# A four-layer Perceiver kernel: ones rows through GpSimd's queue, key tiles cleared three blocks ahead, value copies on ScalarE, queries in four groups

## The chip, the cores and the metric

The kernel runs on one core of a Trainium2 chip. The metric is the device time of one execution in microseconds (us). TensorE is called PE here, VectorE DVE, ScalarE ACT and GpSimd POOL, as in the profile; SyncE (SP) only issues DMA transfers. PEld is TensorE's weight load.

## The reference

A state `x` of 128 rows by 256 passes four layers; each has a cross-attention to 12544 context rows, a self-attention variant and a feed-forward part, and each part's result is added to `x`:

```python
x = x + _L0_xattn_ref(_layernorm(x, axis=-1), ctx_1024, mask_BxS2_ik0, ...)
...
x = x + _L1_xattn_ref(ctx_1024, ctx_1024, _layernorm(x, axis=-1), fside_SxS2_0, fside_BxS2_0, ...)
...
x = x + _L2_xattn_ref(_layernorm(x, axis=-1), ctx_1024, ctx_1024, ...)
...
x = x + _L3_xattn_ref(_layernorm(x, axis=-1), ctx_1024, ctx_1024, mask_Bx1x1xS2_fk0, ...)
```

The four cross-attentions have the same core, with 16 heads of 16 numbers; as layer 0 has it:

```python
q = _split_heads(hidden_states @ q_w.T + q_b)
k = _split_heads(context @ k_w.T + k_b)
v = _split_heads(context @ v_w.T + v_b)
scores = jnp.einsum('bhqd,bhkd->bhqk', q, k) / jnp.sqrt(jnp.float32(HD))
mask = (attention_mask > 0)[:, None, None, :]
scores = jnp.where(mask, -jnp.inf, scores)
probs = jax.nn.softmax(scores, axis=-1)
ctx = jnp.einsum('bhqk,bhkd->bhqd', probs, v)
```

Layer 0 masks keys, layer 1 adds a full 128 x 12544 table and a row to the scores, layer 2 has no mask, layer 3 adds a row. The keys and values of all layers depend on the context alone, not on `x`. Layer 1's self-attention is a delta rule with convolutions, layer 2's a masked attention, and layer 2's feed-forward part is in fixed point with a GELU made of straight pieces.

## The kernel before, in words

The parts are named l0x, l0a, l0f, l1x, ... l3f (x cross-attention, a self-attention, f feed-forward) and run in this order. Everything is float32.

**Projection jobs.** The context's keys and values are projected in small jobs, 50 for keys and 49 for values for each of the four cross-attentions, in one list (`projections`, L155). A context block is 1024 rows (13 blocks, the last of 256); it is loaded by SyncE's queue, 1 MB, into one of two buffers (`load`, L184). A key job makes 128 x 512 keys on PE, ACT moves them from PSUM to SBUF (L209), and after a half block POOL's queue stores them to HBM (L212). A value job makes the values of 256 rows with eight matmuls (L226, run by `mm`, L315). They are copied from PSUM into a staging tile by ACT if `self.side` is set (L232), else by DVE (L234). Two jobs share a staging tile, whose ones columns POOL writes first (L223), and POOL's queue stores it (L237); there are two staging tiles. So a job's parts use PE, ACT or DVE, POOL and two DMA queues.

**Who runs the jobs.** In a cross-attention, as many jobs as the next steps need are run at once, and more by `rate` (0.9 a step in the first pass of l2x and l3x). Outside, `one` (L127) runs `self.share` jobs each time it hands out a PSUM bank; l1_attn, l2_attn and l2_ffn run jobs of later layers so. PSUM's eight banks are handed out in turn (L135).

**A cross-attention** (`cross`, L355). The norm of `x` is transposed, and the queries of all 16 heads are made in one bank, then scaled into four tiles `qb` (L381 to L392), one for each unit of four heads. A unit makes two passes over the keys, 25 steps of 512 keys each: the first takes the maxima of the scores (`score_s`: matmuls L483, DVE maxima L496, or L491 where layer 1 adds its table), the second makes the scores again, transposed, with the maximum taken off (`score_t`: L533), their exponentials on ACT (L546), and products with the values (L588). The second pass trails the first by 27 steps (`lead`), so that during the first 27 steps of a cross-attention there are only score steps and projection jobs (called the first pass below), and later both passes of neighbouring units side by side.

**Key tiles.** A score matmul multiplies 32 rows for a head: a row of ones, a row of the mask, 16 of keys, and zeros. The 17 tiles of 1024 keys by 128 rows (four heads) are made ready by `clear(n)` (L406): POOL zeroes a tile (L409), and SyncE's queue writes the four ones rows (L410, 16 KB). `fetch_k` (L420) is called two steps ahead; for each new block b it runs the jobs up to that block, calls `clear` so that tiles up to b + 2 exist, and issues on SyncE's queue the mask rows (L432) and four loads of keys (L437), and for layer 1 the side table (L442). Each tile is cleared once a cross-attention; later blocks reuse the tiles.

**Order.** The main loop of `cross` runs under a manual schedule: every engine and queue gets its instructions in the order in which the program writes them, and each of them works through its own in that order. Elsewhere the framework orders the instructions.

Of the kernel before, what the change touches and what calls it, by code (L numbers as in the profile page):

```python
# [10 lines left out]
F32 = mybir.dt.float32  # L11
# [7 lines left out]
P = 128  # L19
# [3 lines left out]
SB = 1024  # L23
ST = 512
NSB = -(-S2 // SB)
NST = -(-S2 // ST)
# [51 lines left out]
class Net:  # L78
# [276 lines left out]
    def cross(self, name, side=False, project=True, rate=()):  # L355
# [4 lines left out]
        nc, tc = self.nc, self.tc  # L360
        self.share, self.side = 0.0, side
        width = WIDTH[name]
        units = 16 // width
        lead = NST + 2
        batch = 4 // width
        behind = batch if width == 4 else batch + 1
        with ExitStack() as es:
            pool = es.enter_context(tc.tile_pool(name=f"{name}_p", bufs=1))
# [7 lines left out]
            def rows(u):  # L376

                at = 32 * (width * u % 4)
                return slice(at, at + 32 * width)

            ps = self.bank(f"{name}_q")  # L381
            for g in range(4):
                self.mm(ps[:, g * P : (g + 1) * P], [wq[:, c, g * P : (g + 1) * P] for c in range(2)],
                        [xnT[:, c, :] for c in range(2)])
            qb = []
            for u in range(units):
                g, r = width * u // 4, rows(u)
                q = pool.tile([P, P], F32, name=f"{name}_qb{u}", tag=f"qb{u}")
                nc.vector.tensor_scalar(out=q[r, :], in0=ps[r, g * P : (g + 1) * P],
                                        scalar1=self.col(f"{name}_qb")[r, g : g + 1],  # L390
                                        scalar2=0.25, op0=ALU.add, op1=ALU.mult)
                qb.append(q)  # L392
            lows = []
            for i in range(2):
                low = pool.tile([P, P], F32, name=f"{name}_low{i}", tag=f"low{i}")
# [10 lines left out]
            def clear(n):  # L406
                while len(kts) < min(held, n + 1):
                    t = kp.tile([P, SB], F32, name=f"{name}_kt{len(kts)}", tag=f"kt{len(kts)}")
                    nc.gpsimd.memset(t, 0.0)  # L409
                    nc.sync.dma_start(out=t[0::32, :],  # L410
                                      in_=self.io["ones"][:, :SB].to_broadcast([4, SB]))
                    kts.append(t)
                while len(vts) < nv:
                    n = SB // P * 17 * width
                    t = kp.tile([P, n + 15], F32, name=f"{name}_vt{len(vts)}",
                                tag=f"vt{len(vts)}")
                    nc.gpsimd.memset(t[:, n:], 0.0)
                    vts.append(t)

            def fetch_k(k):  # L420

                u, i = divmod(k, NST)
                if u >= units:
                    return
                s, m = i * ST, min(ST, S2 - i * ST)
                if s % SB == 0:
                    b = s // SB
                    self.until(name, b, "k")
                    n = min(SB, S2 - b * SB)
                    clear(NSB * u + b + 2)  # L430
                    t = kts[(NSB * u + b) % held]
                    nc.sync.dma_start(  # L432
                        out=t[1::32, :n],
                        in_=self.mask_rows[name][:, s : s + n].to_broadcast([4, n]))
                    for j in range(width):
                        at, h = 32 * j + 2, width * u + j
                        nc.sync.dma_start(out=t[at : at + 16, :n],  # L437
                                          in_=self.kx[name, b][16 * h : 16 * h + 16, :])
                    kt[u, b] = t
                if side:  # L440
                    f = ep.tile([P, ST], F32, name=f"{name}_f{k}", tag="f", bufs=3)
                    nc.sync.dma_start(out=f[:, :m], in_=self.io["fside"][:, s : s + m])  # L442
                    ft[k] = f
# [171 lines left out]
            with tc.manual_schedule():  # L615
                for k in (0, 1):
                    fetch_k(k)
                for at in range(total + lead + 3):
                    fetch_k(at + 2)
                    fetch_v(at + 2 - lead)  # L620
                    ke = at - lead if 0 <= at - lead < total else None
                    km = at if at < total else None
                    scores(ke, km)
                    if 0 < at <= total and at % NST == 0:
                        lower(at // NST - 1)


                    left = sum(1 for (n, _, _), _ in self.jobs if n == name)
                    goal = min(n_k, 2 * (at + 6))
                    if at >= lead - 6:  # L630
                        goal = min(n_own, n_k + 2 * (at - lead + 7))
                    self.pump(min(left, max(0, goal - (n_own - left))))
                    phase = max(0, at - 2) // NST
                    due += rate[phase] if phase < len(rate) else 0.0
                    while due >= 1.0:
                        self.pump(1)
                        due -= 1.0


                    while waiting:  # L640
                        u, i = divmod(waiting[0], NST)
                        n = NST - i if NST - i < 2 * batch else batch
                        last = waiting[0] + n - 1
                        if ke is not None and ke - last < behind - batch + 1:
                            break
                        if last > waiting[-1]:
                            break
                        values(waiting[:n])
                        waiting = waiting[n:]
                    if ke is not None:  # L650
                        waiting.append(ke)
                    u, i = divmod(at - lead - 2 - NST, NST)
                    if i == 0 and 0 <= u < units:
                        finish(u)
# [119 lines left out]
    def l1_attn(self):  # L774

        nc = self.nc
        H, HD = 4, 64
        with self.tc.tile_pool(name="l1a", bufs=1) as pool, \
                self.tc.tile_pool(name="l1a_r", bufs=2) as rp:
# [146 lines left out]
            for h, parts in enumerate((((0, 0), (1, 1)), ((1, 2), (2, 3)),  # L926
                                       ((3, 0), (4, 1)), ((4, 2), (5, 3)))):
                q = (h % 2) * HD
# [62 lines left out]
    def l1_ffn(self):  # L991

        nc = self.nc
        E = 8
        with self.tc.tile_pool(name="l1f", bufs=1) as pool, \
                self.tc.tile_pool(name="l1f_h", bufs=2) as hp:
# [67 lines left out]
    def l2_attn(self):  # L1064

        nc = self.nc
        with self.tc.tile_pool(name="l2a", bufs=1) as pool:
            w = self.weight(("w_l2a", None)).rearrange("p (c f) -> p c f", c=2, f=1024)
            xn, xnT = self.normed(pool, "l2a")
            xs = [xnT[:, c, :] for c in range(2)]  # L1070
            qk = []
            for i, nm in enumerate("qk"):
                ps = self.one(f"l2a_{nm}")
                for f in range(2):
                    at = i * D + f * P
                    self.mm(ps[:, f * P : (f + 1) * P], [w[:, c, at : at + P] for c in range(2)],
                            xs)
                t = pool.tile([P, 2, P], F32, name=f"l2a_{nm}T", tag=f"{nm}T")
                nc.vector.tensor_copy(t.rearrange("p c t -> p (c t)"), ps[:, :D])
                qk.append(t)  # L1080
            ps = self.one("l2a_v")
            self.mm(ps[:, :D], xs, [w[:, c, 512:768] for c in range(2)])
            v = pool.tile([P, D], F32, name="l2a_vs", tag="v")
            nc.scalar.copy(v, ps[:, :D])
            ps = self.one("l2a_s")
            self.mm(ps[:, :P], [qk[0][:, c, :] for c in range(2)],
                    [qk[1][:, c, :] for c in range(2)])
            s = pool.tile([P, 1, P], F32, name="l2a_sc", tag="s")
            nc.vector.scalar_tensor_tensor(out=s[:, 0, :], in0=ps[:, :P], scalar=1.0 / 16.0,
                                           in1=self.const("one_ge"), op0=ALU.mult, op1=ALU.mult)  # L1090
            z = pool.tile([P, P], F32, name="l2a_z", tag="z")
            nc.vector.tensor_scalar(out=z, in0=s[:, 0, :], scalar1=0.0, scalar2=-9.0e15,
                                    op0=ALU.is_equal, op1=ALU.mult)
            nc.vector.tensor_tensor(out=s[:, 0, :], in0=s[:, 0, :], in1=z, op=ALU.add)
            self.softmax(pool, s, 1, "l2a")
            aT = self.transposed(pool, s[:, 0, :], "l2a_a")
            ps = self.one("l2a_o")
            self.mm(ps[:, :D], [aT[:, 0, :]], [v])
            self.add_to_x([ps[:, :D]], "l2a")
# [9 lines left out]
    def l2_ffn(self):  # L1109

        nc = self.nc
        with self.tc.tile_pool(name="l2f", bufs=1) as pool, \
                self.tc.tile_pool(name="l2f_r", bufs=3) as rp:
            xn, xnT = self.normed(pool, "l2f")
# [366 lines left out]
```

## Time and profile before

| | us |
|---|---|
| median of 3 runs | 2459.25 (2456.62 to 2461.36) |
| the profiled execution: its time | 2463.49 |
| its span, first to last instruction | 2461.6 |
| mean granted TensorE clock (1 is full) | 0.965 |

The profiled execution is 4.2 us above the median. Where the stages lie in its span, with the busy time of three engines in each stretch:

| stretch, us | what | PE | DVE | ACT | granted clock |
|---|---|---|---|---|---|
| 36 to 170 | l0x, first pass | 126.18 | 69.97 | 29.61 | 0.95 |
| 170 to 465 | l0x, the rest | 294.60 | 226.53 | 149.49 | 1.00 |
| 643 to 745 | l1x, first pass | 94.25 | 72.99 | 17.03 | 0.95 |
| 745 to 1215 | l1x, the rest | 467.29 | 389.20 | 230.95 | 0.99 |
| 1308 to 1427 | l1a | 111.15 | 80.59 | 28.31 | 0.97 |
| 1520 to 1617 | l2x, first pass | 88.36 | 74.75 | 7.73 | 0.92 |
| 1617 to 1842 | l2x, the rest | 224.47 | 195.88 | 150.84 | 1.00 |
| 1905 to 1925 | l2a | 19.95 | 11.15 | 3.83 | 1.00 |
| 1925 to 1982 | l2f | 29.18 | 41.50 | 17.01 | 0.76 |
| 1982 to 2071 | l3x, first pass | 79.15 | 73.03 | 1.58 | 0.84 |
| 2071 to 2297 | l3x, the rest | 225.59 | 197.50 | 150.13 | 0.99 |

In the lines of the profile, "L234 DVE" is the instruction that line 234 of the kernel issues on DVE, "a<-b" gives output and input tiles, and "x4" says how many were put together. In a timeline the first two numbers are start and duration. "[2.02 <-DMA l3x_kt]" says that the engine was idle for 2.02 us before and which event ended that. In lists of waits the numbers are total us, number of waits and the longest. SPq is SyncE's queue.

### The profile page before, as it was taken

The numbers are of one execution on the slowest core, as the hardware profiler recorded it, in microseconds if no ns is written. First come the engines' busy times: TensorE is split into PE (matmuls) and PEld (weight loads), VectorE is DVE, ScalarE is ACT, GpSimd is POOL, SyncE is SP. The second block draws the span as 40 slices with busy tenths as digits, with TensorE's granted clock in tenths as the row PEclk, the third lists the DMA queues.
The fourth block names the chain that finished last, engine by engine and source line by source line (L and its number), as shares of the span: only waits on it lengthen the run. The fifth ranks groups of instructions, "written<-read, shape, count | busy, mean of one in ns | idle before, by whom it ended". The sixth has DMA issues, their size and how long they took to land. (4 is left out here: it accounts for less than half of the span.)

```text
span 2461.6 us, 75645 instructions
## 1 busy us (share of the span) xinstructions
PE 2324.9 (94%) x32103; PEld 1716.3 (70%) x32103; DVE 1628.7 (66%) x3503; ACT 1150.0 (47%) x2109; POOL 246.2 (10%) x465
## 2 busy tenths in 40 slices
PE   6999999999899999999998998899999679999969
PEld 3358888876447876666777744478888546888848
DVE  2566688522477788888886734788882769888331
ACT  2213366773214445545582254046668302666832
POOL 2221100001221100000101111200000121000001
PEclk9999999999999999999999998999999888999979
DMA  7766633237779867777765675553322633333216
GB/s 273 263 222 215 208 97 93 69 118 278 259 232 303 275 216 223 229 227 219 223 198 191 211 254 195 165 151 92 92 78 68 231 109 101 91 91 97 63 44 225
DMA packets 191119, 430.29 MB, mean 175 GB/s; under 512 B 26908, under 2 KB 83248, under 8 KB 186688
## 3 DMA queue, kind: packets, MB, share of 16 engines
q1 hardware_dynamic: 154576, 269.26, 36.9%
q0 software_dynamic: 35840, 154.94, 16.8%
q8 instruction: 256, 4.19, 0.7%
q10 hardware_dynamic: 368, 1.25, 0.1%
q14 instruction: 79, 0.65, 0.1%
HBM read 319.18 MB, written 106.16 MB: 173 GB/s over the span
## 5 line engine op out<-in xcount | busy, mean ns | idle before, releaser
L546 ACT ACTIVATE l1x_e<-l1x_e 128x512 f32<-128x512 f32 (+1 forms) x400 | 240.5, 622 | 248.2 <-DVE l1x_e L541 248.2
L491 DVE CUSTOM_DVE_ANT_0 l1x_j<-l1x_s,l1x_f 128x512 f32<-128x512 f32 (+1 forms) x400 | 271.1, 678 | 80.9 <-PE l1x_t L533 29.9
L496 DVE TENSOR_REDUCE l0x_mxs<-l0x_s 128x1 f32<-128x512 f32 (+1 forms) x400 | 244.3, 672 | 97.5 <-PE l0x_s L483 66.0
L546 ACT ACTIVATE l0x_e<-l0x_t 128x512 f32<-128x512 f32 (+1 forms) x400 | 203.2, 594 | 176.9 <-PE l0x_t L533 173.4
L546 ACT ACTIVATE l3x_e<-l3x_t 128x512 f32<-128x512 f32 (+1 forms) x400 | 203.4, 594 | 167.2 <-PE l3x_s L483 92.6
L496 DVE TENSOR_REDUCE l2x_mxs<-l2x_s 128x1 f32<-128x512 f32 (+1 forms) x400 | 243.8, 672 | 36.7 <-PE l2x_t L533 24.3
L546 ACT ACTIVATE l2x_e<-l2x_t 128x512 f32<-128x512 f32 (+1 forms) x400 | 203.4, 594 | 137.2 <-PE l2x_t L533 133.5
L496 DVE TENSOR_REDUCE l3x_mxs<-l3x_s 128x1 f32<-128x512 f32 (+1 forms) x400 | 243.4, 671 | 33.1 <-PE l3x_t L533 23.9
L541 DVE TENSOR_TENSOR l1x_e<-l1x_t,l1x_g 128x512 f32<-128x512 f32 (+1 forms) x400 | 249.9, 671 | 11.3 <-PE l1x_t L533 8.3
L483 PE MATMUL l3x_s<-l3x_kt,l3x_qb 32*128 32x512 f32 (+1 forms) x800 | 202.8, 652 | 7.1 <-DMA l3x_kt<-l3x_kx 3.5
L533 PE MATMUL l1x_t<-l1x_qb,l1x_kt 32*128 32x128 f32 x3136 | 204.3, 284 | 2.7 <-ACT l1x_vs L232 0.6
L483 PE MATMUL l1x_s<-l1x_kt,l1x_qb 32*128 32x512 f32 (+1 forms) x800 | 203.2, 618 | 3.4 <-DMA l1x_kt<-l1x_kx 3.2
L533 PEld LDWEIGHTS l1x_t<-l1x_qb,l1x_kt 32*128 32x128 f32 x3136 | 171.6, 187 | 36.5 <-ACT l2x_ks L209 19.6
L483 PE MATMUL l2x_s<-l2x_kt,l2x_qb 32*128 32x512 f32 (+1 forms) x800 | 189.5, 620 | 5.8 <-DMA l2x_kt<-l2x_kx 5.3
L483 PE MATMUL l0x_s<-l0x_kt,l0x_qb 32*128 32x512 f32 (+1 forms) x800 | 183.5, 614 | 5.6 <-ACT l0x_ks L209 3.8
L533 PE MATMUL l3x_t<-l3x_qb,l3x_kt 32*128 32x128 f32 x3136 | 181.1, 281 | 0.0
L533 PE MATMUL l2x_t<-l2x_qb,l2x_kt 32*128 32x128 f32 x3136 | 180.0, 280 | 0.0
L533 PE MATMUL l0x_t<-l0x_qb,l0x_kt 32*128 32x128 f32 x3136 | 178.9, 279 | 0.0
L533 PEld LDWEIGHTS l3x_t<-l3x_qb,l3x_kt 32*128 32x128 f32 x3136 | 160.8, 187 | 6.5 <-issue 5.0
L533 PEld LDWEIGHTS l2x_t<-l2x_qb,l2x_kt 32*128 32x128 f32 x3136 | 159.8, 186 | 5.9 <-issue 5.0
L533 PEld LDWEIGHTS l0x_t<-l0x_qb,l0x_kt 32*128 32x128 f32 x3136 | 159.1, 186 | 5.9 <-issue 5.0
L588 PEld LDWEIGHTS l1x_p<-l1x_e,l1x_vt 128*32 128x32 f32 x3136 | 82.0, 110 | 51.3 <-DVE l1x_mxs L491 18.9
(599 smaller groups left out, 3665.8 us busy)
## 6 DMA issues: line engine op xcount, KB each, us to landing
l1x_f<-in_fside SPq DMA_DIRECT2D x96, 256.0 KB
l1x_g<-in_fsideT SPq DMA_DIRECT2D x96, 256.0 KB
w<-in_w_l3f POOLq DMA_DIRECT2D x16, 1024.0 KB, 5.1
l0x_vx<-l0x_vs POOLq DMA_DIRECT2D x24, 544.0 KB, 5.5
l0x_vt<-l0x_vx SPq DMA_DIRECT2D x48, 272.0 KB
l1x_vx<-l1x_vs POOLq DMA_DIRECT2D x24, 544.0 KB, 5.9
l1x_vt<-l1x_vx SPq DMA_DIRECT2D x48, 272.0 KB
l2x_vx<-l2x_vs POOLq DMA_DIRECT2D x24, 544.0 KB, 4.8
```

The costliest lines, as they stand in the source:

```text
L483: nc.tensor.matmul(banks[j][:, :m], qb[u][r, :], t[r, at : at + m], start=True, stop=True)
L491: nc.vector.tensor_tensor_reduce(out=junk[:, :m], in0=banks[j][:, :m], in1=ft[k][:, :m], scale=1.0, scalar=-3.0e38, op0=ALU.add, op1=ALU.m ...
L496: nc.vector.tensor_reduce(out=mxs[u][:, j, i : i + 1], in_=banks[j][:, :m], axis=AX.X, op=ALU.max)
L533: nc.tensor.matmul(banks[j][:, a * P : (a + 1) * P], t[r, at + a * P : at + (a + 1) * P], qb[u][r, :], start=True, stop=True)
L541: nc.vector.tensor_tensor(out=e[:, j, :m], in0=src, in1=gt[k][:, : m // P, :].rearrange("p a q -> p (a q)"), op=ALU.add)
L546: nc.scalar.activation(e[:, j, :m], src, AF.Exp)
L588: nc.tensor.matmul(ps[32 * c : 32 * c + 32, :P], lhs, rhs, start=n < 4, stop=n >= len(todo) - 4, skip_group_check=True)
```

## The change

Four edits, three of them in `cross`:

- The four ones rows of a key tile are issued by POOL's DMA queue, not SyncE's, and tiles exist up to block b + 3.
- The queries are made for a group of four heads at a time, the first ahead of the loop, the others at steps 12, 37 and 62, each in a bank of its own.
- `self.side` is set for each step: in the first 27 steps of l2x and l3x value jobs are copied by ACT (l1x has it set throughout; l0x stays with DVE).
- `self.side` is also set in l1_attn, l2_attn and l2_ffn, and cleared in l1_ffn.

```diff
-            ps = self.bank(f"{name}_q")
-            for g in range(4):
-                self.mm(ps[:, g * P : (g + 1) * P], [wq[:, c, g * P : (g + 1) * P] for c in range(2)],
+            qb = {}
+
+            def query(g):
+                ps = self.bank(f"{name}_q{g}")
+                self.mm(ps[:, :P], [wq[:, c, g * P : (g + 1) * P] for c in range(2)],
                         [xnT[:, c, :] for c in range(2)])
-            qb = []
-            for u in range(units):
-                g, r = width * u // 4, rows(u)
-                q = pool.tile([P, P], F32, name=f"{name}_qb{u}", tag=f"qb{u}")
-                nc.vector.tensor_scalar(out=q[r, :], in0=ps[r, g * P : (g + 1) * P],
-                                        scalar1=self.col(f"{name}_qb")[r, g : g + 1],
+                qb[g] = pool.tile([P, P], F32, name=f"{name}_qb{g}", tag=f"qb{g}")
+                nc.vector.tensor_scalar(out=qb[g], in0=ps[:, :P],
+                                        scalar1=self.col(f"{name}_qb")[:, g : g + 1],
                                         scalar2=0.25, op0=ALU.add, op1=ALU.mult)
-                qb.append(q)
+
+            query(0)
...
-                    nc.sync.dma_start(out=t[0::32, :],
-                                      in_=self.io["ones"][:, :SB].to_broadcast([4, SB]))
+                    nc.gpsimd.dma_start(out=t[0::32, :],
+                                        in_=self.io["ones"][:, :SB].to_broadcast([4, SB]))
...
-                    clear(NSB * u + b + 2)
+                    clear(NSB * u + b + 3)
...
                 for at in range(total + lead + 3):
+                    self.side = side or (at < lead and name != "l0x")
...
                     scores(ke, km)
+                    if at < total - NST and at % NST == 12:
+                        query(at // NST + 1)
...
     def l1_attn(self):
...
+        self.side = True
...
     def l1_ffn(self):
...
+        self.side = False
...
     def l2_attn(self):
...
+        self.side = True
...
     def l2_ffn(self):
...
+        self.side = True
```

## The prediction

> **What bounds the kernel now.** I read the page's busy times and slices first, then busy time by stage, then what TensorE and SyncE's queue wait for, the timeline around stalls, and the chain. From the page and the answer by stage (columns: stretch, length, busy PE, PEld, DVE, ACT, POOL with counts, granted clock, DMA share, GB/s):
>
> ```profile
> PE 2324.9 (94%) x32103; PEld 1716.3 (70%) x32103; DVE 1628.7 (66%) x3503; ACT 1150.0 (47%) x2109; POOL 246.2 (10%) x465
> 1520.00:1617.00 97.00, 88.36 (x392) 46.63 (x396) 74.75 (x129) 7.73 (x11) 22.08 (x34) 0.92 0.52 165
> 1617.00:1842.00 225.00, 224.47 (x5232) 195.94 (x5225) 195.88 (x379) 150.84 (x295) 0.96 (x2) 1.00 0.37 98
> 1925.00:1982.00 57.00, 29.18 (x141) 24.87 (x139) 41.50 (x52) 17.01 (x15) 8.50 (x18) 0.76 0.45 155
> 1982.00:2071.00 89.00, 79.15 (x332) 48.84 (x334) 73.03 (x127) 1.58 (x2) 22.07 (x34) 0.84 0.41 128
> ```
>
> TensorE bounds most of the span, and nearly all of the rest of a cross-attention (second row of stretches). Only first passes (l2x from 1520, l3x from 1982; l1x from 643 has 94.25 busy in 102) and l2f (1925) have slack that this change can reach, and there the clock is down too: each gap of PE is followed by 3.4 to 7 us at half clock. The timeline at a stall of l3x, then SyncE's waits in l2x's and in l3x's first pass:
>
> ```profile
> 1995.21 0.68 DVE L234 COPY l3x_vs<-l3x_v 128x512 f32<-128x512 f32 x1
> 1995.81 2.47 DVE L496 TENSOR_REDUCE l3x_mxs<-l3x_s 128x1 f32<-128x512 f32 x4
> 1996.44 0.75 POOL L237 DMA_DIRECT2D l3x_vx<-l3x_vs  x1 [10.47 <-DVE l3x_vs L234]
> ...
> 1997.18 0.97 POOL L409 MEMSET l3x_kt<- 128x1024 f32 x1
> 1998.17 0.52 SPq L410 DMA_DIRECT2D l3x_kt<-in_ones  x1
> 1999.34 1.77 SPq L437 DMA_DIRECT2D l3x_kt<-l3x_kx  x4
> 2001.72 3.48 PE L483 MATMUL l3x_s<-l3x_kt,l3x_qb 32*128 32x512 f32 x8 [2.02 <-DMA l3x_kt<-l3x_kx]
> ```
>
> ```profile
> SPq L410 <- POOL l3x_vs L223: 25.1, 6, 9.1
> SPq L410 <- POOL l2x_kt L409: 14.9, 5, 5.0
> ```
>
> ```profile
> SPq L410 <- POOL l3x_vs L223: 21.4, 4, 7.9
> SPq L410 <- POOL l3x_kt L409: 12.6, 6, 6.1
> ```
>
> So: VectorE's copy lets POOL store (L237), POOL then clears a tile two blocks ahead (L409), SyncE waits for that with its ones DMA (L410), and the four key loads (L437) of the block wanted two steps (6 us) later stand behind it. The eight products that were late then took 3.48 us, not the 1.14 of a step at full clock.
>
> **What the copies cost by themselves: nothing.** In an undisturbed step of l2x or l3x with a value piece, DVE does a copy and four maxima, 5 x 0.598 from start to start = 2.99 us; PE does scores and job, 1.07 + 1.92 = 2.99. Without the copy PE still needs 2.99. A step with a key job (drained by ScalarE already) takes 2.98. So the gain is only in stalls, stage starts and l2f.
>
> **Stalls (ones rows on POOL's queue, three blocks ahead).** SyncE no longer waits for a clear at its queue's head; a late clear is seen only after three blocks (six steps, 18 us), and the longest wait above is 9.1. Each stall is priced as gap plus slow instructions after it, less a normal step:
> - l2x: near 1560 4.4, 1574 2.4, 1589 7.1 (gap 2.91, scores 3.49 for 1.07, job 3.76 for 1.92), 1609 2.8: 16.7.
> - l3x: 2001 6.2 (2.02 + 2.4 + 1.8), 2019 2.5, 2025 2.3, 2041 to 2045 2.5: 13.5. The last is seven memsets in a row (6.32 us) against a 3.10 us wait of PE.
> - l1x: 4.27 for a context load that SyncE issued late behind the same wait, and 3.2 for key loads: some 7; but there SyncE also waits 9.6 for the side tiles (L442), so half.
>
> What is late next is the context load: 1 MB, two buffers, on the same queue (L184 waited 4.7 in l2x), and loads that now arrive together. I take three quarters of l2x and l3x, 12.5 and 10, and 3.5 for l1x: 26 (12 if such loads take over, 36 if all goes).
>
> **Stage starts.** At l3x:
>
> ```profile
> 1983.93 1.53 SPq L410 DMA_DIRECT2D l3x_kt<-in_ones  x2
> ...
> 1985.12 3.68 PE L315 MATMUL l3x_q<-l3x_xnT,w 128*128 128x128 f32 x16 [0.52 <-DVE l3x_xnT L302]
> ...
> 1988.84 1.13 DVE L389 TENSOR_SCALAR l3x_qb<-l3x_q,cols 128x128 f32<-128x128 f32 x4 [3.77 <-PE l3x_q L315]
> ```
>
> 16 query instructions at half clock, four scalings, and key loads behind the clearing of three tiles. Afterwards: a quarter of the queries (0.92, plus 0.34), ones off SyncE. The first scores then wait for the key loads: from start to landing these move up by the two clears and ones DMAs, 2.3 in l0x, 2.5 in l1x, 2.0 in l2x, 1.2 in l3x: 8.0 (5 to 10). The three later query groups cost PE 3 x 4 instructions a stage (0.23 at half clock, so 0.115) = 1.4, in stretches that it bounds: 5.6 back. Their scalings (0.34) lie beside PE.
>
> **68 ones DMAs on POOL.** No row shows a 16 KB transfer there. Key stores issue in 0.54 there, value stores in 0.75, beside VectorE at its maxima; 17 x 0.54 = 9 us a stage on an engine busy 22 of 97 is covered by the 18 us of lead; uncovered is only the first tile. Here a rule speaks against the change: the Trainium skill ("SBUF — State Buffer", SBUF: two separate sides) says that a transfer from GpSimd's queue is held while VectorE is in a two-port mode, some 3.1 us for 0.62. By the rule the first ones row of each stage would be 2.5 late, up to 10 in four stages, and the starts would gain nothing; by the row it is 0.5 and covered by the loads behind it. At the starts VectorE runs the norm for a few us only. I take the row; the rule stays as the low end of the starts.
>
> **Copies on ScalarE.** Bounds by the row of L232: some 0.57 from start to start, against 0.60 to 0.69 on VectorE. Steps of first passes: nothing, as shown; ScalarE is busy 7.73 of 97 and 1.58 of 89. In l2a PE is busy 19.95 of 20: nothing. In l1a PE waits 4.8 for copies at 1336, but POOL's staging memset had come 5.60 us late behind the store's landing, which stays: 2 (0 to 8). In l2f the end is set by VectorE's polynomial; the chain:
>
> ```profile
> 1931.18 17.71 PE l3x_v L315 x82
> 1948.89 25.41 issue
> 1974.30 5.70 PE l2f_o L315 x16
> ```
>
> PE has nothing to do for 25.4 us. VectorE's chain of 43 us (1931.2 to 1974.3) holds 11 copies (11 x 0.6 = 6.6) and a wait of a copy for its staging tile, 4.83: without them some 32. But ScalarE makes the terms: 15 Relus of 1.15 (L1144), now with 11 copies of 0.57 between them, and a copy that waits for staging holds them. 11 less 5: 6 (3 to 10).
>
> **Sum.** Stalls 26, starts 8.0, queries -5.6, l1a 2, l2f 6: 36.4 less. The profiled run took 2463.5 (span 2461.6), 4.2 above the median; 2463.5 - 36.4 = 2427.1, on the median's scale 2422.9.
>
> **Rivals.**
> - Smaller gain: key loads then wait for the context loads instead. For: L184's 4.7, a 2.6 us wait of PE for a context tile in l2x. Against: SyncE's waits for POOL are eight times L184's in l2x. Stalls give 5 to 15, l2f and l1a 5 to 8: 2436 to 2452, 2443 in the middle.
> - It does not do what it says: the ones rows queue behind the same value stores on POOL, only one block later, and PE sets the step with or without copies. What remains is starts less queries, 2.4, and losses alike: 2457. For: 9.1 us waits for staging are POOL's own; against: one block is 6 us.
> - Slower: ScalarE's queue order. Copies that wait for a staging tile stand ahead of the stage's own ScalarE work. In l1a 29 copies x 0.57 = 16.5, if each lies in the chain of products and ScalarE copies (L884); in l2f, with all 15 Relus behind the last copy (1952.9), 0.7 + 17.3 to the last Relu and 6.9 from there to the end make 1977.8, 3.5 later. Together 20; it decides where the stalls give under 17.6 (20 less the 2.4 of starts and queries); with none, 2459.3 + 17.6 = 2477. Against: PE runs l1a gaplessly from 1345, so it is a bound there before ScalarE.
>
> **Chances.** Near the sum 0.62 (2410 to 2435), smaller gain 0.20, no effect 0.08, slower 0.10. What a measurement of this kernel can tell from no change is 0.2%, 4.9 us: half of the no-effect case lies in it. Faster 0.62 + 0.20 + 0.02 = 0.84, same 0.04, slower 0.02 + 0.10 = 0.12. The range takes the first case with its costs' ends and most of the second: 2408 to 2449.
>
> **What would show it.** SyncE's waits for POOL in first passes near zero; the l2x first pass from 97 to some 84, l3x from 89 to 80, with clocks above 0.92 and 0.84; steps of scores and a value piece still at 2.98; queries as four groups of 0.46 to 0.92; the 25.4 us of l2f at 19. I am wrong if PE's waits for key loads stay, now ended by POOL or behind L184, if first scores wait for a ones row, or if l1a's window grows.

## The result, and the profile after

The changed kernel takes 2418.4 us (median of 4 runs, 2417.5 to 2425.0), the kernel before 2458.1 on the same chip: ratio 0.9843, 95% interval 0.9822 to 0.9863, 39.7 us less by the medians. The forecast was 2423, 36.4 less. On another chip, run once more beside the last experiments, the ratio was 0.9841 (0.9818 to 0.9863).

First the page's busy times, then the answer by stage for l2x's first pass, its rest, l2f, and l3x's first pass, of the changed kernel (columns as before):

```profile
PE 2303.4 (95%) x32103; PEld 1703.5 (71%) x32103; DVE 1583.2 (66%) x3429; ACT 1190.5 (49%) x2183; POOL 288.9 (12%) x533
1506.00:1586.00 80.00, 79.16 (x378) 41.29 (x378) 66.30 (x114) 14.07 (x23) 33.64 (x54) 0.96 0.67 209
1586.00:1812.00 226.00, 225.59 (x5226) 196.50 (x5229) 196.34 (x381) 152.09 (x296) 1.20 (x3) 1.00 0.34 94
1895.00:1950.00 55.00, 30.10 (x142) 25.53 (x140) 34.66 (x39) 22.88 (x29) 8.18 (x18) 0.78 0.50 164
1952.00:2026.00 74.00, 72.22 (x322) 46.06 (x324) 63.58 (x110) 8.32 (x13) 30.85 (x48) 0.80 0.47 146
```

PE's gaps are gone in l2x (busy 79.16 of 80, before 88.36 of 97) and nearly gone in l3x (72.22 of 74, before 79.15 of 89). In l2x POOL's busy time went from 22.08 to 33.64, and nothing waits for it. l2f hardly got shorter, though VectorE has 7 us less to do there.

One sign that the forecast named did not come: l3x's granted clock is 0.80, not above 0.84. In the last 16 us of its first pass no job is left; VectorE, with the maxima, is busy 15.86 us and the clock is 0.50. Before, it was 0.50 in the last 13 us too. Why it is low there is not shown.

What SyncE waits for in the two first passes, l2x and then l3x:

```profile
SPq L184 <- PE l3x_k L315: 12.6, 3, 6.9
SPq L184 <- PE l3x_v L315: 12.0, 3, 5.6
```

```profile
SPq L184 <- PE l3x_v L315: 11.7, 2, 6.5
SPq L432 <- POOL l3x_kt L409: 6.1, 2, 5.7
```

The 40.0 and 34.0 us for POOL are gone in l2x and down to 6.1 in l3x. What comes last now is the context load (L184), which waits until PE has used up a buffer; PE in turn waits 0 us for key loads in l2x and 1.6 in l3x (before 5.3, and in l3x 3.5 and 3.1 for a clear). The timeline of a step with a value piece in l2x:

```profile
1574.24 1.14 PE L483 MATMUL l2x_s<-l2x_kt,l2x_qb 32*128 32x512 f32 x8
1575.23 0.81 POOL L237 DMA_DIRECT2D l3x_vx<-l3x_vs  x1 [3.69 <-ACT l3x_vs L232]
1575.31 1.99 PE L315 MATMUL l3x_v<-l3x_kvw,l3x_cv 128*128 128x256 f32 x8
...
1575.59 0.53 SPq L432 DMA_DIRECT2D l2x_kt<-in_ones  x1
1576.04 0.97 POOL L409 MEMSET l2x_kt<- 128x1024 f32 x1
1576.16 1.84 SPq L437 DMA_DIRECT2D l2x_kt<-l2x_kx  x3
...
1577.30 0.56 POOL L410 DMA_DIRECT2D l2x_kt<-in_ones  x1 [0.29 <-POOL l2x_kt L409]
```

SyncE issues mask row and keys while POOL is still clearing: before, the same clear stood ahead of them. A ones row costs POOL 0.56 to issue, about what a key store does (0.54).

Measured by stretch in the two profiled executions (these differ by 46 us, more than the medians; some of that is luck: l3f, where nothing was changed, was 2.5 shorter, at a clock of 0.94 against 0.90):

| term | forecast less | measured less, before to after |
|---|---|---|
| l2x, first scores to end of first pass | 12.5 | 14.2 (92.20 to 77.96) |
| l3x, the same | 10 | 11.1 (82.25 to 71.19) |
| l1x, the same | 3.5 | 4.7 (102.84 to 98.14) |
| l0x, the same | 0 | 2.7 (140.8 to 138.1) |
| starts, norm to first scores: l0x, l1x, l2x, l3x | 2.3, 2.5, 2.0, 1.2 | 0.4, -0.2, 3.2, 2.0 |
| query groups | -5.6 | -1.4, 1.3, -1.2, -1.0 in the rest of l0x, l1x, l2x, l3x |
| l1a | 2 | 4.4 (118.04 to 113.65) |
| l2a | 0 | 1.4 |
| l2f | 6 | 1.5 (57.09 to 55.62) |

### The profile page after: what moved, and what is told of

It is laid out like the page before. It is cut to its first block, busy times and chain, and to the rows that moved or that the text cites. A ratio compares the mean times of both kernels' runs of the same rounds, so it can differ in the third digit from the quotient of the medians.

```text
span 2415.4 us, 75731 instructions
## 1 busy us (share of the span) xinstructions
PE 2303.4 (95%) x32103; PEld 1703.5 (71%) x32103; DVE 1583.2 (66%) x3429; ACT 1190.5 (49%) x2183; POOL 288.9 (12%) x533
## 3 DMA queue, kind: packets, MB, share of 16 engines
q10 hardware_dynamic: 368, 1.25, 0.1%
## 4 chain that ended last, share of the span: by engine, by line
PE 33%; issue 13%; DMA 2%; DVE 2%; ACT 1%; POOL 0%; SPq 0%; DVEq 0%; POOLq 0%; ACTq 0%
PE l3x_t L533 5%; PE l3x_p L588 4%; PE l3x_s L483 4%; PE l3x_k L315 4%; PE l2x_v L315 3%; PE l3x_v L315 2%; PE l2x_s L483 1%; PE l1x_t L533 1%; DMA l3x_vx<-l3x_vs 1%; PE l3f_h L315 1%; PE l1x_p L588 1%; PE l3f_o L315 1%; PE l1f_h L315 1%; PE l1f_o L315 1%; ACT l1x_e L546 1%
## 5 line engine op out<-in xcount | busy, mean ns | idle before, releaser
L496 DVE TENSOR_REDUCE l2x_mxs<-l2x_s 128x1 f32<-128x512 f32 (+1 forms) x400 | 243.8, 672 | 39.7 <-PE l2x_t L533 25.1
L496 DVE TENSOR_REDUCE l3x_mxs<-l3x_s 128x1 f32<-128x512 f32 (+1 forms) x400 | 243.0, 672 | 36.2 <-PE l3x_t L533 24.6
```

What stands on the lines that cost most here:

```text
L496: nc.vector.tensor_reduce(out=mxs[u][:, j, i : i + 1], in_=banks[j][:, :m], axis=AX.X, op=ALU.max)
```

## The experiments

Ratios are to the kernel before on the same chip, with 95% intervals; 0.001 is 2.5 us. Single times of one kernel lie up to 21 us from its median, and the intervals reach 3 to 7 us to either side, so that smaller differences are not told apart.

**One part alone.** First the ones rows on POOL's queue and the third block:

```diff
-                    nc.sync.dma_start(out=t[0::32, :],
+                    nc.gpsimd.dma_start(out=t[0::32, :],
...
-                    clear(NSB * u + b + 2)
+                    clear(NSB * u + b + 3)
```

> Only the ones rows on POOL's queue and clearing three blocks ahead; queries and copies as before. Theory (the stalls came from SyncE's key loads standing behind a ones row that waited for POOL's clear): the first passes of l2x and l3x lose their stalls, some 12 and 10 us, l1x 4; the stage starts gain nothing in l2x and l3x, since there all queries are still made first, l0x 1 to 2: together 25 to 29 less. Rival 1 (the key loads then stand behind context loads, or the stores are still too late without the copies on ScalarE): 5 to 12 less. Rival 2 (the change does its work by taking the copies off VectorE): under 5 less.

Ratio 0.9847 (0.9818 to 0.9877), 35.7 less by the medians: nearly the whole effect, and more than the theory's 25 to 29. The answer by stage for the first passes of l2x and l3x shows why the copies aren't needed for it:

```profile
1514.00:1594.00 80.00, 79.04 (x386) 41.75 (x386) 72.67 (x128) 7.72 (x11) 33.30 (x54) 0.98 0.69 209
1967.00:2042.00 75.00, 74.51 (x330) 47.56 (x332) 69.74 (x122) 0.00 (x0) 30.52 (x48) 0.80 0.48 143
```

VectorE still makes the copies (ACT has 0.00 in l3x), and the first passes are as short as in the changed kernel: 75.87 and 71.39 from first scores to end, against 77.96 and 71.19. Rivals 1 and 2 fall.

Then only the copies in the first passes:

```diff
                 for at in range(total + lead + 3):
+                    self.side = side or (at < lead and name != "l0x")
```

> Only the copies by ScalarE in the first 27 steps of l2x and l3x. Theory: PE sets a step at 2.98 us with or without the copy on VectorE; the stores to HBM come up to 2.5 us earlier, so that the waits behind them shrink but stay: 3 to 9 less, in l2x and l3x only, and SyncE's waits for POOL stay at 20 us or more a stage. Rival (VectorE's relief is what shortened the first passes): 22 to 26 less.

Ratio 0.9980 (0.9967 to 0.9994), 1.5 to 8 us less: the theory's size. SyncE still waits 23.8 and 16.8 us for POOL in l2x.

Then only the copies in l1a, l2a and l2f:

```diff
     def l1_attn(self):
...
+        self.side = True
...
     def l1_ffn(self):
...
+        self.side = False
...
     def l2_attn(self):
...
+        self.side = True
...
     def l2_ffn(self):
...
+        self.side = True
```

> Only the copies by ScalarE in l1a, l2a and l2f. Theory from the two traces: l1a 4.4 less, l2a 1.4, l2f 1.5, since in l2f the Relus stand behind copies that wait for a staging tile: together 6 to 8 less. Rival (as forecast): l2f 6, l1a 2: the same sum, but l2f's stretch at 51. Rival (ScalarE's order costs in l1a): 0 or slower.

Ratio 0.9979 (0.9967 to 0.9991), 5.7 less by the medians. The sum is just under the theory's 6 to 8. In its profile l1a is 5.3 shorter (112.79), l2a 1.6 and l2f 2.1 (54.98), but l1a's share is not settled by that: in the next run, which leaves these copies with VectorE, l1a took 110.3. ScalarE's order shows no cost in l1a: it waits there for staging tiles (15.2 us in the changed kernel's l1a, where VectorE waited 8.3 before) and has time for it, being busy 43 of 114.

Then only the query groups:

```diff
+            query(0)
...
                     scores(ke, km)
+                    if at < total - NST and at % NST == 12:
+                        query(at // NST + 1)
```

> Only the queries by group. Theory: the first key loads, still behind three clears and ones rows, let the first scores start at most 1 us earlier in l2x and l3x and not at all in l0x and l1x, and the groups moved into the loop cost 1.4 a stage: 2 to 5 slower, which can hardly be told from no change. Rival (the queries set the start): 5 to 9 less at the four starts, 0 to 3 less in all.

Ratio 1.0047 (1.0029 to 1.0065), 8.6 slower by the medians, more than the theory's 2 to 5. Its profile (2461.4) was the fastest of its 18 runs, so it can't show all of this. It shows the starts of scores 0.7 to 1.9 earlier, 0.8 to 1.3 more in the later passes of l0x, l2x and l3x, and first passes that lose 5.0 in l0x and 6.4 in l2x, where PE waits 6.7 for key loads (before 5.3). Why the stalls grew stays open.

**Parts undone in the changed kernel.** Ones rows back on SyncE's queue, three blocks ahead:

```diff
-                    nc.gpsimd.dma_start(out=t[0::32, :],
+                    nc.sync.dma_start(out=t[0::32, :],
```

> The changed kernel with the ones rows back on SyncE's queue, still three blocks ahead. Theory (what mattered is that SyncE's queue no longer stands at a wait for POOL's clear): the ones row of block b + 3 waits at the head of SyncE's queue for a clear that was only just written, so the key loads of block b stand behind it as before: of the 39.7 gained, 15 to 27 are lost, 2433 to 2446, and SyncE waits again 20 us or more for POOL in the first passes of l2x and l3x. Rival (the lead of one block more is what did it): within 5 of the changed kernel's 2418.

Ratio 1.0032 (1.0019 to 1.0045): all of the gain is lost, and some 8 us with it, where 15 to 27 lost were expected. In the profile the four first passes are 41 longer than in the changed kernel, and the starts 7.4. Why it ends above the kernel before stays open; the query groups alone had cost 8.6 with the ones rows on this queue. This kernel's waits of SyncE in l2x, from the end of l1f on:

```profile
SPq L410 <- POOL l3x_vs L223: 23.1, 5, 10.0
...
SPq L410 <- POOL l2x_kt L409: 17.6, 9, 6.0
SPq L184 <- PE l3x_v L315: 4.4, 1, 4.4
```

The waits are those of before. In its l3x the order can be seen:

```profile
2001.33 0.97 POOL L409 MEMSET l3x_kt<- 128x1024 f32 x1
...
2002.32 0.53 SPq L410 DMA_DIRECT2D l3x_kt<-in_ones  x1
...
2003.49 1.77 SPq L437 DMA_DIRECT2D l3x_kt<-l3x_kx  x4
...
2005.96 2.42 PE L483 MATMUL l3x_s<-l3x_kt,l3x_qb 32*128 32x512 f32 x8 [0.45 <-DMA l3x_kt<-l3x_kx]
```

The ones row of a later block stands at the queue's head until POOL has cleared the tile, however far ahead that tile's use is, and the key loads of the block that is needed next stand behind it.

Tiles only two blocks ahead, the ones rows on POOL's queue:

```diff
-                    clear(NSB * u + b + 3)
+                    clear(NSB * u + b + 2)
```

> The changed kernel with tiles cleared two blocks ahead, ones rows on POOL's queue. Theory: two blocks are 12 us, more than the longest wait for POOL of 9.1, and SyncE has nothing to wait for: within 5 of 2418, 2414 to 2424. Rival (the lead counts): 2428 or more, with PE's waits in l2x and l3x ended by POOL or by a ones row.

Ratio 0.9823 (0.9803 to 0.9844), median 2417.9: no difference from the changed kernel. With the run before this settles it: the queue is the cause, and with the rows on POOL's queue the third block adds nothing.

All queries first, the rest as changed:

```diff
-            query(0)
...
-                    if at < total - NST and at % NST == 12:
-                        query(at // NST + 1)
```

(with the old loop over four groups in place of `query`)

> The changed kernel without the query groups: all queries first, as before. Theory by the part tried alone (8 to 16 slower than before): the groups cost more than they give here too: 2406 to 2415. Rival (with the key loads early, the queries set the start of l2x and l3x): starts 1.4 to 2.5 later there, moved groups 1.4 cheaper in each of four stages: 2415 to 2420, no difference.

Ratio 0.9825 (0.9804 to 0.9845), median 2418.3: no difference; the rival holds. In its profile l2x's first scores start 2.6 later and l3x's 0.7, and the rest of l0x, l1x, l2x and l3x is 1.4, 2.0, 1.3 and 1.3 shorter. So in the whole time the groups take later what they give at the starts.

VectorE for the copies in l2f alone:

```diff
     def l2_ffn(self):
...
-        self.side = True
+        self.side = False
```

> The changed kernel with VectorE making the copies in l2f, as before. Theory: with ScalarE its Relus wait for copies that wait for staging, with VectorE its own chain is longer by the copies; the two cost nearly the same: l2f's stretch 55 to 58, 0 to 2 slower. Rival (as forecast): 6 slower.

Ratio 0.9877 (0.9857 to 0.9897); its runs (2425.2 to 2430.1) lie all above those of the changed kernel on that chip (2414.4 to 2422.7), 8.1 by the medians. So the theory from one profile was too low. Its profile shows only part: l2f 1.5 longer (57.02 against 55.55 in the changed kernel there), and the stretch from l2a's norm to l2f's 1.3 (19.35 against 18.05). All profiles together are clearer: l2f takes 57.0 to 61.9 in the five where VectorE copies (58.4 in the mean), 51.4 to 55.7 in the nine where ScalarE does (54.3). The 8.1 fits badly with the 5.7 that all three stages gave alone; 4 to 8 is what the runs leave, and the forecast's 6 lies in it.

**What holds l2f.** The chain of the changed kernel, and the timeline around the longest wait in it:

```profile
1905.51 9.00 DMA l3x_vx<-l3x_vs
...
1917.26 7.51 DMA l3x_vx<-l3x_vs
```

```profile
1904.63 0.89 POOL L264 DMA_DIRECT2D w<-in_w_l3a  x1
...
1905.51 0.80 POOL L237 DMA_DIRECT2D l3x_vx<-l3x_vs  x1
...
1914.61 0.59 ACT L232 COPY l3x_vs<-l3x_v 128x512 f32<-128x512 f32 x1 [5.10 <-DMA l3x_vx<-l3x_vs]
1915.10 1.15 ACT L1151 ACTIVATE l2f_k<-l2f_a,kinks 128x1024 f32<-128x1024 f32 x1
...
1916.28 1.23 DVE L1152 SCALAR_TENSOR_TENSOR l2f_y<-l2f_k,l2f_y 128x1024 f32<-128x1024 f32 x1 [4.15 <-ACT l2f_k L1151]
```

A copy waits 5.10 for a store to free its staging tile; the Relu behind it on ScalarE waits with it, and VectorE 4.15 for the Relu. The stores take up to 9 us; this one was issued on POOL's queue right behind a weight load of 1 MB. Two ways to take that away were tried. Three staging tiles (paid for in layer 1's tables):

```diff
-                t["v"] = self.bp.tile([P, u, 4, 17 * wd], F32, name=f"{name}_vs{b}_{a}", tag="vst")
+                t["v"] = self.bp.tile([P, u, 4, 17 * wd], F32, name=f"{name}_vs{b}_{a}", tag="vst", bufs=3)
...
-                    f = ep.tile([P, ST], F32, name=f"{name}_f{k}", tag="f", bufs=3)
+                    f = ep.tile([P, ST], F32, name=f"{name}_f{k}", tag="f", bufs=2)
...
-                qb[g] = pool.tile([P, P], F32, name=f"{name}_qb{g}", tag=f"qb{g}")
+                qb[g] = pool.tile([P, P], F32, name=f"{name}_qb{g}", tag=f"qb{g % 3}")
```

> The changed kernel with three staging tiles for values in place of two; to make room, layer 1's side tables have two buffers in place of three, and the query tiles of units 0 and 3 are one. Theory (in l2f ScalarE's Relus stood behind copies that waited for a staging tile, 5.1 and 2.9 us in the trace): l2f's stretch goes from 55.6 to 45 to 49, its waits of ScalarE for the stores to near 0, l1a 0 to 3 less: 2407 to 2413, if layer 1 loses nothing by its tables. Rival (the stores only come late by the DMA queues, and three tiles wait as long): l2f within 2 of 55.6.

Ratio 0.9898 (0.9881 to 0.9915), worse: l1x lost 16.1 in its first pass and 8.6 later, where SyncE waits for a free table (45.9 us for VectorE, 36.3 in the changed kernel), and l2f kept 54.5. A copy still waited 5.65, and one Relu with it. The theory fails; the rival's size holds.

Two weight loads on ScalarE's queue:

```diff
-            self.nc.gpsimd.dma_start(out=t[:, : src.shape[1]], in_=src)
+            queue = self.nc.scalar if name in ("w_l1a1", "w_l3a") else self.nc.gpsimd
+            queue.dma_start(out=t[:, : src.shape[1]], in_=src)
```

> The changed kernel with two weight loads of 1 MB (the second of layer 1's self-attention, and that of layer 3's) issued by ScalarE's queue in place of POOL's. Theory (on POOL's queue small transfers stand behind a weight load: at l1x's start the first ones row was issued at 637.7 and awaited until 644.5, with a weight load issued at 635.5; in l2f a value store took 9.0 us with one issued right ahead of it): l1x's first scores start 2 to 3 us earlier, l2f goes from 55.6 to 50 to 53: together 4 to 8 less than the changed kernel on this chip. Rival (the DMA engines share, whatever the queue): under 2 less, store and ones row land as late.

Ratio 0.9832 (0.9810 to 0.9854), median 2416.9 against 2418.3 for the changed kernel there: not told apart. l2f was 51.4 in the profile, but it was 51.8 in the kernel shown next too, where the weight loads had stayed on POOL's queue: l2f moves by 4 us without an edit there. Whether the queue behind a weight load costs l2f anything is not settled.

**The start of l1x.** Next, only the first tile's ones row on SyncE's queue:

```diff
-                    nc.gpsimd.dma_start(out=t[0::32, :],
+                    (nc.gpsimd if kts else nc.sync).dma_start(
```

> The changed kernel with the ones row of each stage's first tile on SyncE's queue, the other 16 on POOL's. Theory: l1x's first scores start 2 to 3 us earlier, since the first row no longer stands behind a weight load; the other starts lose 0 to 0.5 (one more issue of 0.5 ahead of the key loads): 0 to 3 less in all, hardly to be told. Rival (the key loads or the side table set l1x's start): no difference there, 1 to 2 slower.

Ratio 0.9849 (0.9826 to 0.9872), median 2420.1: no difference. What PE's first scores waited for in l1x, in the changed kernel, with two weight loads moved, and with the first ones row moved:

```profile
PE l1x_s L483 <- DMA l1x_kt<-in_ones: 4.9, 1, 4.9
```

```profile
PE l1x_s L484 <- DMA l1x_kt<-l1x_kx: 3.6, 1, 3.6
```

```profile
PE l1x_s L483 <- DMA l1x_kt<-in_pad: 2.8, 1, 2.8
```

Each time another transfer came last. From the norm's scaling to the scores it took 7.1, 6.4 and 6.4, and 6.0 in the changed kernel's second profile, so that neither move shows an effect. Why all that was issued there landed late was not found.

Last, the changed kernel once more:

> The changed kernel once more, for comparison on the same chip: 0.982 to 0.986 of the kernel before.

Ratio 0.9841 (0.9818 to 0.9863).

## Why the prediction was right, and where it was off

- **The main step held:** SyncE's key loads stood behind a ones row that waited for POOL. That part alone has a ratio of 0.9847 where the whole has 0.9843, and with the row back on SyncE's queue nothing is left.
- **Its second half was not needed.** The forecast put part of the effect on the third block (18 us of lead). Two blocks do as well.
- **Copies in steps of the first passes:** nothing, as worked out; in the kernel with the ones rows alone a step with VectorE's copy is 1.07 + 1.92 again. Taken alone they gave 1.5 to 8 us with the old queue; that earlier stores did this is argued, not shown.
- **Stalls, 26:** mis-sized low, and l0x was put at nothing without a reason. The two profiles show 32.7 with l0x (14.2 + 11.1 + 4.7 + 2.7). All fourteen profiles divide by the queue of the ones rows, whatever else was edited (the table under this list). The sum there, 35.3, is close to what the ones rows gave alone (35.7). The context loads were expected to take a quarter of the gain; SyncE waits 24.6 us for their buffers in l2x, but PE not once. (The terms' upper end, 36, should be 37: 16.7 + 13.5 + 7.)
- **Stage starts, 8.0:** 5.4 in the profiles (0.4 - 0.2 + 3.2 + 2.0), and 2.2 of these have a cause that the forecast did not have: the norm's scaling, with which the stretch begins, takes less itself (0.68 less in l1x, 0.67 in l2x, 0.83 in l3x; see the last section). In l0x and l1x, 2.3 and 2.5 forecast, the profiles show no gain. In l1x "these move up" holds for the issues, 1.8 earlier against the queries' start (L432 0.4 after it before, 1.4 ahead of it now), but not for the landings: the scores began 1.6 after the last key load was issued before, 4.6 now. First scores that wait for a ones row, named as a sign of being wrong, came there, in one of the two profiles of the changed kernel. In l0x the key loads were issued 2.2 sooner after the second key store, but that store came 1.2 later in this execution.
- **Queries, -5.6:** nearly right. By all profiles the groups cost 1.2 to 1.5 in the rest of l0x, l2x and l3x; in l1x no cost stands out.
- **l1a, 2:** 4.4 in the two profiles, within the 0 to 8, but not settled. With VectorE's copies l1a takes 110.3 to 118.7 (four profiles, 116.0 in the mean), with ScalarE's 109.9 to 114.8 (ten, 113.1). PE's wait of 4.8 for copies is gone, but it was also absent with the query groups alone. l2a, put at 0, gives about 1.
- **l2f, 6:** 4 to 8 by the runs, 1.5 in the first two profiles; PE's idle time there fell from 25.4 to 22.4, not to 19. The wait for staging did move onto ScalarE, ahead of its Relus, as the rival had it, and costs less than VectorE's copies did.
- **The rule on POOL's queue:** no run shows it. The ones rows issue in 0.56. The one that came late, at l1x's start, came while VectorE had nothing to do (idle from 640.0 to 646.5), so it was not held by a VectorE mode.
- **Luck:** stalls came out higher than forecast, starts lower, and these errors partly cancel. The sum is nearer than its terms.

| first pass, us | SyncE's queue, 5 profiles | POOL's queue, 9 profiles (one with the first row on SyncE's) | less, by the means |
|---|---|---|---|
| l0x | 140.8 to 145.8 | 136.8 to 139.8 | 5.2 |
| l1x | 102.0 to 105.6 | 98.1 to 99.6 (three staging tiles: 114.2) | 4.2 |
| l2x | 91.1 to 98.5 | 75.9 to 79.9 | 16.5 |
| l3x | 78.1 to 82.2 | 70.2 to 73.6 | 9.4 |

## What to carry to other kernels

A transfer that must wait for an engine is worth trying on that engine's own queue, where it is in order anyway, if that engine has time for it (POOL was busy 34 of 80 us). On a shared queue its wait was paid by everything behind it, and issuing it earlier didn't help. Copies that an engine makes while another sets the pace are worth nothing to move, unless a store or a chain hangs on them. A few us in one profile of a stage are not an effect: l2f moved by 4 us and l1a by 8 between kernels that agree there. The ranges over all profiles tell more.

## What the hardware showed unasked

The norm's scaling at the start of a stage (L288) got faster with no edit to it. In the kernel before, the changed one, and the one with the first ones row on SyncE's queue:

```profile
1517.84 1.08 DVE L288 TENSOR_SCALAR l2x_xn<-l1f_x,l2x_mv,l2x_r 128x256 f32<-128x256 f32 x1
```

```profile
1504.62 0.41 DVE L288 TENSOR_SCALAR l2x_xn<-l1f_x,l2x_mv,l2x_r 128x256 f32<-128x256 f32 x1
```

```profile
1503.48 1.84 POOL L409 MEMSET l2x_kt<- 128x1024 f32 x2
1504.39 1.08 DVE L288 TENSOR_SCALAR l2x_xn<-l1f_x,l2x_mv,l2x_r 128x256 f32<-128x256 f32 x1
```

Where POOL clears tiles one after the other, the instruction is 0.67 us longer; where POOL turns to a DMA issue after the first tile, it isn't. It was so in l1x and l2x of the kernels looked at, and in l3x, where it took 1.24 and 1.25 against 0.41. This agrees in part with the Trainium skill ("SBUF — State Buffer", SBUF: two separate sides): VectorE in a two-port mode and GpSimd share a port pair as an exclusive lock, and whichever starts second waits for the other's whole instruction. In direction it agrees, but the whole rule is not seen: 0.67 is less than a clearing (0.97), and in the changed kernel's l3x the instruction starts at 1950.47, by the records 0.21 before the first clearing ends, and still takes 0.41. That VectorE's instruction ran in a mode that needs the shared pair is inferred from the time, not shown.
